# Keeping x by channel through two attention layers: strips and 32x32 turns on VectorE

## The chip, the cores and the metric

The kernel runs on one core of a Trainium2 chip. The metric is the device time of one execution in microseconds (us); before the change the median of 3 runs is 3623.92 us (3623.29 to 3624.22). Engines are named as in the profile: PE is TensorE's matrix multiply and PEld its weight load, DVE is VectorE, ACT is ScalarE, POOL is GpSimd, SP is SyncE, whose queue issues most of the transfers.

## The reference, cut to what matters

x has 128 rows (`s`) of 256 positions with 256 channels, in fp32. Two layers follow one another; each normalizes x in 32 groups of 8 channels over the whole tensor, runs attention within each row, and adds the result to x.

```python
def _gn(v, G=32, eps=1e-5):            # statistics over rows, positions and the 8 channels of a group
    B_, H_, W_, C_ = v.shape
    g = v.reshape(B_, H_, W_, G, C_ // G)
    m = jnp.mean(g, axis=(1, 2, 4), keepdims=True)
    s = jnp.var(g, axis=(1, 2, 4), keepdims=True)
    return ((g - m) / jnp.sqrt(s + eps)).reshape(v.shape)

# layer 0: 8 heads of 32, a bias from pair_repr added after the softmax, and a gate
#   bias = pair_repr @ bias_proj ; gate = sigmoid(xn @ gate_proj) ; q, k, v = xn @ qkv_proj
#   attend = (softmax(q k^T * scale) + bias) v * gate ; out = attend @ out_proj
x = x + _L0_conv_ref(_gn(x), pair_repr, gate_proj, qkv_proj, out_proj, bias_proj)
# layer 1: 4 heads of 64, q, k, v with bias, only keys within 16 positions
#   y = softmax(masked(q k^T / 8)) v @ w_out.T + b_out
x = x + _L1_conv_ref(_gn(x), w_in, b_in, w_out, b_out, 16)
```

The second layer's statistics need all of the first layer's output, so the layers are two passes with x1, the sum after layer 0, kept in DRAM between them.

## The kernel before

The tensors are called here as in the profile: `xg` and `yg` are four rows of x or x1 in SBUF, `px` their transpose in PSUM, `xn` the normalized row by channel, `po` and `1po` the output products, `o` and `1o` the sums that are stored. A prefix `1` marks layer 1.

First comes an early stage: pair_repr is loaded (32 MB), turned and multiplied into the bias table, while all of x (33.5 MB) passes through for the statistics of layer 0. Weights are loaded in one transfer each; w_in and w_out are transposed once on PE.

```python
qkv_sb = const.tile([P, 2, 3 * C], F32, name="qkv_sb")
nc.scalar.dma_start(out=qkv_sb, in_=qkv_w.rearrange("(t p) o -> p t o", p=P))
# ... gate_sb, out_sb the same way, one transfer each; bqk, bv, bo
w_nat = st_pool.tile([P, 8, C], F32, name="w_nat")
nc.scalar.dma_start(out=w_nat[:, 0:6, :], in_=w_in.rearrange("(t p) c -> p t c", p=P))
nc.scalar.dma_start(out=w_nat[:, 6:8, :], in_=w_out.rearrange("(t p) c -> p t c", p=P))
# ... 16 transposes of w_nat on PE into w_in_t, w_out_t; then the loop over pair_repr and x
```

Then each row of each layer. A row arrives with positions on the partitions and must have channels there for the products, so PE transposes it:

```python
def normalized(pool, xg, mean, rstd, name):
    px = proj_bank(f"px{name}")
    for half in range(2):
        for t in range(2):
            nc.tensor.transpose(                                                    # L300
                px[:, half, t * P : (t + 1) * P], xg[:, t, half * P : (half + 1) * P], ident
            )
    xn = pool.tile([P, 2, R], F32, tag="xn", name=f"xn{name}")
    for half in range(2):
        nc.vector.tensor_scalar(                                                    # L305
            xn[:, half, :], px[:, half, :],
            mean[:, half : half + 1], rstd[:, half : half + 1], op0=ALU.subtract, op1=ALU.mult,
        )
    return xn

# by_channel (L317): out[channel, position], weights stationary, xn moving (q, k, gate)
# by_token   (L328): out[position, channel], xn or at stationary, weights moving (v, out)
# each: 4 matmuls 128x128 by 256 columns

def rows(ap, s0, n):                                   # 1 KB pieces: 256 channels of one position
    return ap[s0 : s0 + n].rearrange("s (t p) c -> p s t c", p=P)

# layer 0, in a software pipeline of half rows:
#   even half: scores, q, k of row s+1, normalized(s+2), attend
#   odd half : scores, v, gate of row s+1, finish(s-1), attend
def finish(s):                                         # layer 0
    po = by_token(st[s]["at"], out_sb, 0, f"po{s}")
    # ...
    nc.vector.tensor_tensor(o[:, k], po, xgs[s // XG][:, s % XG], ALU.add)          # L453
    if k == SG - 1:                                    # every 8 rows
        nc.sync.dma_start(out=rows(x1, g * SG, SG), in_=o)
        flat = o.rearrange("p s t c -> p (s t) c")
        for j in range(G):                             # 32 groups
            nc.vector.bn_stats(out=stats1[:, j, g, :], in_=flat[:, :, j * CG : (j + 1) * CG])   # L458
# after the layer: group_columns folds stats1 [P, 32, 16, 6] into mean1, rstd1 (L131 to L170)

def finish(s):                                         # layer 1
    po = by_token(st[s]["at"], w_out_t, 0, f"1po{s}", sim_bank)
    # ...
    nc.vector.tensor_tensor(o[:, k], po, bo.unsqueeze(1).to_broadcast([P, 2, C]), ALU.add)      # L601
    nc.gpsimd.tensor_tensor(o[:, k], o[:, k], xgs[g][:, k], ALU.add)                # L602
    if k == XG - 1:                                    # every 4 rows
        nc.sync.dma_start(out=rows(out[0], g * XG, XG), in_=o)
```

Of the kernel before, what the change touches and what calls it, by code (L numbers as in the profile page):

```python
# [15 lines left out]
P = 128  # L16
# [6 lines left out]
BAND = 16  # L23
KB = 64
# [9 lines left out]
def conv_preact_kernel(  # L34
# [45 lines left out]
    nc.scalar.dma_start(out=bias_w_sb[:, 0:H0], in_=bias_w)  # L80
    qkv_sb = const.tile([P, 2, 3 * C], F32, name="qkv_sb")
    nc.scalar.dma_start(out=qkv_sb, in_=qkv_w.rearrange("(t p) o -> p t o", p=P))
    gate_sb = const.tile([P, 2, C], F32, name="gate_sb")
    nc.scalar.dma_start(out=gate_sb, in_=gate_w.rearrange("(t p) o -> p t o", p=P))
    out_sb = const.tile([P, 2, C], F32, name="out_sb")
    nc.scalar.dma_start(out=out_sb, in_=out_w.rearrange("(t p) o -> p t o", p=P))
# [10 lines left out]
    bo = const.tile([P, C], F32, name="bo")  # L97
    nc.scalar.dma_start(out=bo, in_=b_out.partition_broadcast(P))
# [16 lines left out]
    nc.gpsimd.tensor_copy(seen[KB:P], seen_high[KB:P])  # L115

# [7 lines left out]
    def group_columns(pool, stats, sizes, which):  # L124


        tri = stats.rearrange("p g n (e k) -> p g (n e) k", k=3)
        n, total = tri.shape[2], sum(sizes)
        share = pool.tile([P, n], F32, name=f"share{which}")
        for m, size in enumerate(sizes):  # L130
            nc.gpsimd.memset(share[:, 2 * m : 2 * m + 2], size / (2.0 * total))  # L131
        share = share.unsqueeze(1).to_broadcast([P, G, n])
        dev = pool.tile([P, G, n], F32, name=f"dev{which}")
        nc.vector.tensor_tensor(dev, tri[:, :, :, 1], share, ALU.mult)
        means = pool.tile([P, G], F32, name=f"means{which}")
        nc.vector.tensor_reduce(means, dev, axis=AX.X, op=ALU.add)
        nc.vector.tensor_tensor(dev, tri[:, :, :, 1], means.unsqueeze(2).to_broadcast([P, G, n]), ALU.subtract)
        nc.vector.tensor_tensor(dev, dev, dev, ALU.mult)
        nc.vector.tensor_tensor(dev, dev, share, ALU.mult)
        nc.vector.scalar_tensor_tensor(  # L140
            dev, tri[:, :, :, 2], 1.0 / total, dev, op0=ALU.mult, op1=ALU.add
        )
        within = pool.tile([P, G], F32, name=f"within{which}")
        nc.vector.tensor_reduce(within, dev, axis=AX.X, op=ALU.add)
        ps_m = proj_bank(f"ps_m{which}")
        nc.tensor.matmul(ps_m[:, 0, 0:G], lhsT=avg, rhs=means, start=True, stop=True)
        d = pool.tile([P, G], F32, name=f"d{which}")
        nc.vector.tensor_tensor(d, means, ps_m[:, 0, 0:G], ALU.subtract)
        v = pool.tile([P, G], F32, name=f"v{which}")
        nc.vector.tensor_tensor(v, d, d, ALU.mult)  # L150
        nc.vector.tensor_tensor(v, v, within, ALU.add)
        wide = pool.tile([P, 2, G, CG], F32, name=f"wide{which}")
        nc.vector.tensor_copy(wide[:, 0], means.unsqueeze(2).to_broadcast([P, G, CG]))
        nc.vector.tensor_copy(wide[:, 1], v.unsqueeze(2).to_broadcast([P, G, CG]))
        flat = wide.rearrange("p k g c -> p k (g c)")
        ps_c = proj_bank(f"ps_c{which}")
        for k in range(2):
            for half in range(2):
                nc.tensor.matmul(
                    ps_c[:, 0, 2 * k + half : 2 * k + half + 1],  # L160
                    lhsT=flat[:, k, half * P : (half + 1) * P],
                    rhs=avg[:, 0:1],
                    start=True, stop=True,
                )
        mean = const.tile([P, 2], F32, name=f"mean{which}")
        nc.vector.tensor_copy(mean, ps_c[:, 0, 0:2])
        std = pool.tile([P, 2], F32, name=f"std{which}")
        nc.scalar.activation(std, ps_c[:, 0, 2:4], AF.Sqrt, bias=eps)
        rstd = const.tile([P, 2], F32, name=f"rstd{which}")
        nc.vector.reciprocal(rstd, std)  # L170
        return mean, rstd
# [20 lines left out]
    with ExitStack() as early:  # L192
# [6 lines left out]
        nc.scalar.dma_start(out=w_nat[:, 0:6, :], in_=w_in.rearrange("(t p) c -> p t c", p=P))  # L199
        nc.scalar.dma_start(out=w_nat[:, 6:8, :], in_=w_out.rearrange("(t p) c -> p t c", p=P))  # L200
        for o4 in range(2):
            for kt in range(2):
                pw = proj_bank(f"pw{o4}_{kt}").rearrange("p a b -> p (a b)")
                for j in range(4):
                    nc.tensor.transpose(
                        pw[:, j * P : (j + 1) * P], w_nat[:, 4 * o4 + j, kt * P : (kt + 1) * P], ident
                    )
                if o4 == 0:
                    nc.scalar.copy(w_in_t[:, kt, 0:512], pw)
                else:  # L210
                    nc.scalar.copy(w_in_t[:, kt, 512:768], pw[:, 0:256])
                    nc.scalar.copy(w_out_t[:, kt, :], pw[:, 256:512])
# [82 lines left out]
    def normalized(pool, xg, mean, rstd, name):  # L295

        px = proj_bank(f"px{name}")
        for half in range(2):
            for t in range(2):
                nc.tensor.transpose(  # L300
                    px[:, half, t * P : (t + 1) * P], xg[:, t, half * P : (half + 1) * P], ident
                )
        xn = pool.tile([P, 2, R], F32, tag="xn", name=f"xn{name}")
        for half in range(2):
            nc.vector.tensor_scalar(  # L305
                xn[:, half, :], px[:, half, :],
# [5 lines left out]
    def by_channel(w, col, xn, name):  # L312

        ps = proj_bank(name)
# [8 lines left out]
    def by_token(a, w, col, name, bank=proj_bank):  # L323

        ps = bank(name)
# [7 lines left out]

    def rows(ap, s0, n):
        return ap[s0 : s0 + n].rearrange("s (t p) c -> p s t c", p=P)

    x1 = dram.tile([S, R, C], F32, name="x1")
    SG = min(8, S)
# [5 lines left out]
    with ExitStack() as lay:  # L344
        st1 = lay.enter_context(tc.tile_pool(name="st1", bufs=1))
        stats1 = st1.tile([P, G, S // SG, 6], F32, name="stats1")
        with ExitStack() as lay0:
# [6 lines left out]
            def load(g):  # L354
                if g * XG < S:
                    xg = big.tile([P, XG, 2, C], F32, tag="xg", name=f"xg{g}", bufs=3)
                    nc.sync.dma_start(out=xg, in_=rows(x[0], g * XG, XG))
                    xgs[g] = xg

            def piece(s, n):  # L360
                if s >= S:
                    return
                if n == 0:
                    if s % XG == 0:
                        load(s // XG + 1)
                    st[s] = {"xn": normalized(row, xgs[s // XG][:, s % XG], mean0, rstd0, f"0_{s}")}
# [78 lines left out]
            def finish(s):  # L445
                if s < 0:
                    return
                po = by_token(st[s]["at"], out_sb, 0, f"po{s}")
                g, k = divmod(s, SG)
                if k == 0:  # L450
                    outs[g] = big.tile([P, SG, 2, C], F32, tag="o", name=f"o{g}")
                o = outs[g]
                nc.vector.tensor_tensor(o[:, k], po, xgs[s // XG][:, s % XG], ALU.add)  # L453
                if k == SG - 1:
                    nc.sync.dma_start(out=rows(x1, g * SG, SG), in_=o)
                    flat = o.rearrange("p s t c -> p (s t) c")
                    for j in range(G):
                        nc.vector.bn_stats(out=stats1[:, j, g, :], in_=flat[:, :, j * CG : (j + 1) * CG])  # L458
# [22 lines left out]
        mean1, rstd1 = group_columns(st1, stats1, [SG * 2 * CG] * (S // SG), 1)  # L481
# [4 lines left out]
    with ExitStack() as lay:  # L486
# [6 lines left out]
        def load(g):  # L493
            if g * XG < S:
                xg = big.tile([P, XG, 2, C], F32, tag="xg", name=f"yg{g}")
# [97 lines left out]
        def finish(s):  # L593
            if s < 0:
                return
            po = by_token(st[s]["at"], w_out_t, 0, f"1po{s}", sim_bank)
            g, k = divmod(s, XG)
            if k == 0:
                outs[g] = big.tile([P, XG, 2, C], F32, tag="o", name=f"1o{g}", bufs=2)
            o = outs[g]  # L600
            nc.vector.tensor_tensor(o[:, k], po, bo.unsqueeze(1).to_broadcast([P, 2, C]), ALU.add)  # L601
            nc.gpsimd.tensor_tensor(o[:, k], o[:, k], xgs[g][:, k], ALU.add)  # L602
            if k == XG - 1:
                nc.sync.dma_start(out=rows(out[0], g * XG, XG), in_=o)
# [33 lines left out]
    with tc.If(sure < P):  # L638
        with ExitStack() as lay:
# [12 lines left out]
            stats2 = one.tile([P, G, NX, 6], F32, name="stats2")  # L652
# [57 lines left out]
            def again(layer, s, src, dst, mean, rstd):  # L710
                x2 = two.tile([P, 1, 2, C], F32, tag="x2", name=f"x2_{layer}")
                nc.sync.dma_start(out=x2, in_=src[bass.ds(s, 1)].rearrange("s (t p) c -> p s t c", p=P))
                xn = normalized(two, x2[:, 0], mean, rstd, f"2_{layer}")
# [30 lines left out]
                po = by_token(at, out_sb if layer == 0 else w_out_t, 0, f"po2_{layer}")  # L744
                o = two.tile([P, 1, 2, C], F32, tag="o2", name=f"o2_{layer}")
                nc.vector.tensor_tensor(o[:, 0], po, x2[:, 0], ALU.add)
                if layer == 1:
                    nc.vector.tensor_tensor(o[:, 0], o[:, 0], bo.unsqueeze(1).to_broadcast([P, 2, C]), ALU.add)
                nc.sync.dma_start(out=dst[bass.ds(s, 1)].rearrange("s (t p) c -> p s t c", p=P), in_=o)

            with tc.For_i(0, S, 1) as s:
                again(0, s, x[0], x1, mean0, rstd0)
            for n in range(NX):
                x_stats(stats2, x_load(two, x1, n, "2_"), n)
            mean2, rstd2 = group_columns(one, stats2, [k * CG for k in PARTS], 2)
            with tc.For_i(0, S, 1) as s:
                again(1, s, x1, out[0], mean2, rstd2)
# [25 lines left out]
```

## Time and profile before

| stage | from, to (us) | what it does |
|---|---|---|
| early | 0 to 230 | pair_repr and x pass through; bias table and first statistics |
| layer 0 | 230 to 2331 | 128 rows, 16.21 us for one in the steady stretch |
| between | 2333 to 2360 | statistics of x1, first rows of x1 read back |
| layer 1 | 2360 to 3612 | 128 rows, 9.70 us for one |
| end | 3612 to 3621 | last sums and their store |

The stage limits are read from the timeline; 16.21 us is the distance from one row's q product to the next one's, 9.70 us likewise. A row of the view by groups gives line, engine, operation, output and inputs with their shapes, the number of instructions, then busy time, mean ns of one, and the idle time before them with what ended it. A row of the timeline gives start, length, engine, line and what was done; instructions of one kind in a row are merged, and a bracket gives the idle time before and its releaser. A row of the view by windows gives a stretch, its length, and the busy time of each engine in it, then the granted PE clock, the DMA engines' busy share and GB/s.

### The profile page before, as it was taken

To read this page: it belongs to the slowest core of one execution; us is meant where nothing else is said; L and a number is where in the kernel's file an instruction comes from. 1 tells how busy PE (TensorE), PEld (TensorE's weight loads), DVE (VectorE), ACT (ScalarE), POOL (GpSimd) and SP (SyncE) were. 2 spreads that over 40 slices of the span, in tenths; PEclk is the share of its full clock that TensorE was granted. 3 is DMA by queue.
4 is the path that set the end of the run, shared out by engine and by line. 5 is a ranking of instruction groups with operands and counts; after the bars stand their busy time and mean duration, and the time that the engine had idled before them with its cause. 6 is when DMAs were issued, how large, how long until landed. Compare 5 with 4: busy or idle time off the path is not lost. (4 is left out here: it accounts for less than half of the span.)

```text
span 3621.4 us, 92043 instructions
## 1 busy us (share of the span) xinstructions
PE 3472.4 (96%) x40870; PEld 2703.5 (75%) x40870; DVE 2497.3 (69%) x4353; ACT 1404.4 (39%) x3181; POOL 402.3 (11%) x310
## 2 busy tenths in 40 slices
PE   5769999999999999999999999799999999999998
PEld 4457777777777777777777777488888888888887
DVE  5766776776777677677677677756666666666666
ACT  2334444444444444444444444333333333333332
POOL 0000000000000000000000000023333333333332
PEclk8879999999999999999999999899999999999999
DMA  9930110110111011011011010011211211211211
GB/s 332 350 125 13 48 36 13 48 36 14 47 36 48 13 36 48 13 48 36 13 48 36 15 45 25 25 59 49 72 49 49 72 49 48 72 48 49 72 49 37
DMA packets 154051, 209.85 MB, mean 58 GB/s; under 512 B 2992, under 2 KB 135856, under 8 KB 152496
## 3 DMA queue, kind: packets, MB, share of 16 engines
q1 hardware_dynamic: 150800, 201.34, 17.2%
q8 instruction: 323, 5.29, 0.6%
q10 hardware_dynamic: 2848, 2.56, 0.3%
q14 instruction: 80, 0.66, 0.1%
HBM read 136.78 MB, written 67.11 MB: 56 GB/s over the span
## 5 line engine op out<-in xcount | busy, mean ns | idle before, releaser
L397 ACT ACTIVATE ex<-sim 128x512 f32<-128x512 f32 x1024 | 528.6, 603 | 128.3 <-PE sim L390 127.5
L551 POOL TENSOR_TENSOR 1p<-1ex,seen 128x768 f32<-128x768 f32 x128 | 232.3, 1815 | 2514.0 <-ACT 1ex L549 2514.0
L439 DVE RECIPROCAL d<-d 128x256 f32<-128x256 f32 x256 | 445.8, 1741 | 0.0
L305 DVE TENSOR_SCALAR xn<-px,mean,rstd 128x256 f32<-128x256 f32 x512 | 254.8, 539 | 261.6 <-PE px L300 258.9
L587 DVE RECIPROCAL 1rz<-1z 128x512 f32<-128x512 f32 x128 | 428.1, 3344 | 7.3 <-ACT 1z L585 7.3
L435 DVE TENSOR_TENSOR t<-bv,z 128x256 f32<-128x256 f32 x256 | 108.0, 422 | 460.0 <-ACT z L433 460.0
L433 ACT ACTIVATE z<-avz 128x256 f32<-128x256 f32 x256 | 98.1, 383 | 750.1 <-PE avz L428 740.5
L400 DVE TENSOR_TENSOR both<-ex 128x512 f32<-128x512 f32 x512 | 329.0, 682 | 3.0 <-ACT ex L397 3.0
L390 PE MATMUL sim<-q,k 32*128 32x256 f32 x4096 | 293.3, 400 | 0.0
L415 PE MATMUL avz<-ex,v 128*32 128x256 f32 x4096 | 274.8, 385 | 10.5 <-DVE t L436 10.5
L512 ACT ACTIVATE 1q<-p1q,bqk 128x256 f32<-128x256 f32 x256 | 107.5, 470 | 429.5 <-PE p1q L317 429.5
L422 PE MATMUL bv<-bias_sb,v 128*32 128x256 f32 x4096 | 268.9, 379 | 1.1 <-DVE t L435 1.1
L390 PEld LDWEIGHTS sim<-q,k 32*128 32x128 f32 x4096 | 184.9, 184 | 110.5 <-issue 104.9
L317 PE MATMUL pq<-xn,qkv_sb 128*128 128x256 f32 x1024 | 257.0, 394 | 1.5 <-DVE xn L305 1.4
L328 PE MATMUL pv<-qkv_sb,xn 128*128 128x256 f32 x1024 | 255.1, 392 | 0.0
L328 PE MATMUL po<-out_sb,at 128*128 128x256 f32 x1024 | 247.2, 382 | 6.6 <-DVE at L442 4.9
L520 PEld LDWEIGHTS p1v<-w_in_t,xn 128*64 128x64 f32 x4096 | 221.0, 137 | 42.4 <-issue 42.4
L520 PE MATMUL p1v<-w_in_t,xn 128*64 128x128 f32 x4096 | 251.9, 276 | 0.0
L328 PE MATMUL 1po<-w_out_t,1at 128*128 128x256 f32 x1024 | 243.0, 380 | 3.1 <-DVE 1at L589 3.1
L317 PE MATMUL p1q<-xn,w_in_t 128*128 128x256 f32 x1024 | 243.5, 381 | 0.6 <-DVE xn L305 0.6
L317 PE MATMUL pk<-xn,qkv_sb 128*128 128x256 f32 x1024 | 243.2, 380 | 0.0
L317 PE MATMUL p1k<-xn,w_in_t 128*128 128x256 f32 x1024 | 241.9, 379 | 0.0
(105 smaller groups left out, 5368.0 us busy)
## 6 DMA issues: line engine op xcount, KB each, us to landing
xg<-in_x_dram SPq DMA_DIRECT2D x32, 1024.0 KB, 7.8
x<-o SPq DMA_DIRECT2D x16, 2048.0 KB, 8.4
yg<-x SPq DMA_DIRECT2D x32, 1024.0 KB, 8.9
out_dram<-1o SPq DMA_DIRECT2D x32, 1024.0 KB, 5.3
xs<-in_x_dram SPq DMA_DIRECT2D x7, 4096.0 KB, 20.7
xs<-in_x_dram SPq DMA_DIRECT2D x1, 3072.0 KB, 18.8
xs<-in_x_dram SPq DMA_DIRECT2D x1, 1024.0 KB, 9.7
qkv_sb<-in_L_conv_qkv_proj_dram ACTq DMA_DIRECT2D x1, 768.0 KB, 4.6
```

Source lines behind the costliest of these rows:

```text
L305: nc.vector.tensor_scalar(xn[:, half, :], px[:, half, :], mean[:, half : half + 1], rstd[:, half : half + 1], op0=ALU.subtract, op1=ALU.mult,)
L317: nc.tensor.matmul(ps[:, m, :], lhsT=w[:, kt, col + m * P : col + (m + 1) * P], rhs=xn[:, kt, :], start=(kt == 0), stop=(kt == 1),)
L328: nc.tensor.matmul(ps[:, t, :], lhsT=a[:, kt, t * P : (t + 1) * P], rhs=w[:, kt, col : col + C], start=(kt == 0), stop=(kt == 1),)
L390: nc.tensor.matmul(sims[j][:, kt, :], lhsT=k[p0 : p0 + D0, half, kt * P : (kt + 1) * P], rhs=q[p0 : p0 + D0, half, :], start=True, stop=True,)
L397: nc.scalar.activation(ex[:, j], sims[j], AF.Exp, scale=1.0 / math.sqrt(D0))
L400: nc.vector.tensor_tensor(both[:, j : j + 2], ex[:, j : j + 2, 0, :], ex[:, j : j + 2, 1, :], ALU.add)
L415: nc.tensor.matmul(avz[ps, 0, :], lhsT=v[:, kt, ch], rhs=ex[:, j, kt, :], start=(kt == 0), stop=(kt == 1),)
L422: nc.tensor.matmul(bv0[ps, :], lhsT=v[:, kt, ch], rhs=bias_sb[:, kt, 4 * half + j, :], start=(kt == 0), stop=(kt == 1),)
L439: nc.vector.reciprocal(d, d)
L520: nc.tensor.matmul(ps[KB * half : KB * (half + 1), b, :], lhsT=xn[:, kt, KB * b : KB * (b + 1)], rhs=w_in_t[:, kt, 2 * C + P * half : 2 * ...
L551: nc.gpsimd.tensor_tensor(p.rearrange("p j b q -> p j (b q)"), ex.rearrange("p j b q -> p j (b q)"), seen.rearrange("p b q -> p (b q)").un ...
L587: nc.vector.reciprocal(rz, z)
```

## The change

x is kept with channels on the partitions in both layers. It is loaded in four strips of 64 channels, each to 32 partitions; VectorE turns 32x32 blocks within the strips, after which partition 32a+r holds channels 64a+r (half 0) and 64a+32+r (half 1). The weights' rows are ordered in the same way when they are loaded. Output products come out by channel, so that the residual is added by channel, x1 is stored by channel, and the statistics of layer 1 are one pair of values per partition. Layer 1 loads x1 ready for use; its result is turned back by VectorE before it is stored in strips. The aim is to have no transposes of x on PE. A fallback path that runs only on out-of-range softmax sums is changed in the same way and left out below.

```diff
+A, B = 4, 32
+    def by_strip(ap):
+        return ap.rearrange("(a h r) o -> a r h o", a=A, h=2)
+    def strip(a):
+        return slice(B * a, B * (a + 1))
-    nc.scalar.dma_start(out=qkv_sb, in_=qkv_w.rearrange("(t p) o -> p t o", p=P))
-    nc.scalar.dma_start(out=gate_sb, in_=gate_w.rearrange("(t p) o -> p t o", p=P))
+    for a in range(A):
+        nc.scalar.dma_start(out=qkv_sb[strip(a)], in_=by_strip(qkv_w)[a])
+        nc.scalar.dma_start(out=gate_sb[strip(a)], in_=by_strip(gate_w)[a])
-    nc.scalar.dma_start(out=out_sb, in_=out_w.rearrange("(t p) o -> p t o", p=P))
+    for kt in range(2):
+        for h in range(2):
+            nc.scalar.dma_start(
+                out=out_sb[:, kt, h * P : (h + 1) * P].rearrange("p (a r) -> p a r", a=A),
+                in_=out_w.rearrange("(t p) (a h r) -> t h p a r", p=P, a=A, h=2)[kt, h],
+            )
-    bo = const.tile([P, C], F32, name="bo")           # one transfer, broadcast
+    bo = const.tile([P, 2], F32, name="bo")           # four transfers, one for each strip
-        nc.scalar.dma_start(out=w_nat[:, 0:6, :], in_=w_in.rearrange("(t p) c -> p t c", p=P))
+        for t in range(6):
+            for h in range(2):
+                nc.scalar.dma_start(
+                    out=w_nat[:, t, h * P : (h + 1) * P].rearrange("p (a r) -> p a r", a=A),
+                    in_=w_in.rearrange("(t p) (a h r) -> t h p a r", p=P, a=A, h=2)[t, h],
+                )
...
+    def channel_columns(pool, stats, which):
+        mv = pool.tile([P, 2, 2], F32, name=f"mv{which}")
+        for half in range(2):
+            nc.vector.bn_aggr(out=mv[:, half, :], in_=stats[:, half].rearrange("p n s -> p (n s)"))
+        # ... two products with `within` (1/8 inside a group), six small VectorE operations,
+        # ... a square root and a reciprocal on [P, 2]: mean, rstd
...
-    def normalized(pool, xg, mean, rstd, name):
-        px = proj_bank(f"px{name}")
-        ... four nc.tensor.transpose
+    def normalized(pool, xt, mean, rstd, name):
         for half in range(2):
             nc.vector.tensor_scalar(
-                xn[:, half, :], px[:, half, :],
+                xn[:, half, :], xt[:, half, :],
...
+    def in_strips(ap, s0, n, a):
+        return ap[s0 : s0 + n].rearrange("s (b t) (a c) -> a t (s b) c", t=B, a=A)[a]
+    def turned(dst, src, k):
+        for half in range(2):
+            nc.vector.transpose(
+                out=dst[:, half, :].rearrange("p (b t) -> p b t", t=B),
+                in_=src[:, k * (R // B) : (k + 1) * (R // B), half * B : (half + 1) * B],
+            )
-    x1 = dram.tile([S, R, C], F32, name="x1")
+    x1 = dram.tile([S, 2, P, R], F32, name="x1")
     def rows(ap, s0, n):
-        return ap[s0 : s0 + n].rearrange("s (t p) c -> p s t c", p=P)
+        return ap[s0 : s0 + n].rearrange("s h p q -> p s h q")
# layer 0
-                    nc.sync.dma_start(out=xg, in_=rows(x[0], g * XG, XG))
+                    for a in range(A):
+                        nc.sync.dma_start(out=xg[strip(a)], in_=in_strips(x[0], g * XG, XG, a))
-                    st[s] = {"xn": normalized(row, xgs[s // XG][:, s % XG], mean0, rstd0, f"0_{s}")}
+                    xt = row.tile([P, 2, R], F32, tag="xt", name=f"xt{s}", bufs=5)
+                    turned(xt, xgs[s // XG], s % XG)
+                    st[s] = {"xt": xt, "xn": normalized(row, xt, mean0, rstd0, f"0_{s}")}
-                po = by_token(st[s]["at"], out_sb, 0, f"po{s}")
+                po = by_channel(out_sb, 0, st[s]["at"], f"po{s}")
-                nc.vector.tensor_tensor(o[:, k], po, xgs[s // XG][:, s % XG], ALU.add)
+                nc.vector.tensor_tensor(o[:, k], po, st[s]["xt"], ALU.add)
+                if k % 2 == 1:
+                    for half in range(2):
+                        nc.vector.bn_stats(out=stats1[:, half, s // 2, :], in_=o[:, k - 1 : k + 1, half, :])
-                    for j in range(G):
-                        nc.vector.bn_stats(out=stats1[:, j, g, :], in_=flat[:, :, j * CG : (j + 1) * CG])
# layer 1
-            po = by_token(st[s]["at"], w_out_t, 0, f"1po{s}", sim_bank)
+            po = by_channel(w_out_t, 0, st[s]["at"], f"1po{s}", sim_bank)
-            nc.vector.tensor_tensor(o[:, k], po, bo.unsqueeze(1).to_broadcast([P, 2, C]), ALU.add)
-            nc.gpsimd.tensor_tensor(o[:, k], o[:, k], xgs[g][:, k], ALU.add)
+            for half in range(2):
+                nc.vector.scalar_tensor_tensor(
+                    ot[:, half, :], po[:, half, :], bo[:, half : half + 1], xgs[g][:, k, half, :],
+                    op0=ALU.add, op1=ALU.add,
+                )
+                nc.vector.transpose(
+                    out=outs[g][:, k * (R // B) : (k + 1) * (R // B), half * B : (half + 1) * B],
+                    in_=ot[:, half, :].rearrange("p (b t) -> p b t", t=B),
+                )
-                nc.sync.dma_start(out=rows(out[0], g * XG, XG), in_=o)
+                for a in range(A):
+                    nc.sync.dma_start(out=in_strips(out[0], g * XG, XG, a), in_=outs[g][strip(a)])
```

## The prediction, made before the changed kernel ran

> **What bounds the kernel now.** I read busy time by engine first, then the stretches of the two layers, then the timeline of one row in each, and last the edges between stages.
>
> ```profile
> PE 3472.4 (96%) x40870; PEld 2703.5 (75%) x40870; DVE 2497.3 (69%) x4353; ACT 1404.4 (39%) x3181; POOL 402.3 (11%) x310
> ```
>
> ```profile
> 0.00:200.00 200.00, 128.31 (x864) 90.66 (x864) 128.66 (x398) 56.95 (x98) 5.99 (x38) 0.86 1.03 341
> 230.00:2330.00 2100.00, 2082.67 (x19958) 1506.93 (x19958) 1470.28 (x2908) 926.76 (x2050) 0.00 (x0) 1.00 0.10 31
> 2360.00:3610.00 1250.00, 1243.39 (x19957) 1093.26 (x19957) 853.40 (x894) 415.93 (x1025) 394.10 (x255) 1.00 0.17 53
> ```
>
> Stretch, then PE, PEld, DVE, ACT, POOL, clock, DMA share, GB/s. PE is busy 99% of both layers at full clock; VectorE is at 70% and 68%, DMA at 10% and 17%. The early stage is another matter: DMA is saturated there (share 1.03, 341 GB/s). So in the layers time taken off PE is time off the end, as long as nobody else becomes late; in the early stage only bytes and DMA pauses count.
>
> A busy PE hides gaps between instructions, so I price the transposes from starts. PE's timeline in a layer-0 row, then in a layer-1 row with VectorE's division:
>
> ```profile
> 1006.75 1.89 PE L317 MATMUL pk<-xn,qkv_sb 128*128 128x256 f32 x8
> 1008.48 0.60 PE L300 MATMUL px<-ident,xg 128*128 128x128 f32 x4
> 1009.01 1.07 PE L415 MATMUL avz<-ex,v 128*32 128x256 f32 x16
> ...
> 1015.94 1.89 PE L328 MATMUL po<-out_sb,at 128*128 128x256 f32 x8
> 1017.76 1.07 PE L415 MATMUL avz<-ex,v 128*32 128x256 f32 x16
> ```
>
> ```profile
> 2956.36 0.66 PE L300 MATMUL px<-ident,yg 128*128 128x128 f32 x4
> 2956.86 1.89 PE L328 MATMUL 1po<-w_out_t,1at 128*128 128x256 f32 x8
> ...
> 2961.77 0.68 DVE L589 TENSOR_TENSOR 1at<-1avz,1rz 128x512 f32<-128x512 f32 x1
> ...
> 2964.74 0.79 PE L570 MATMUL 1avz<-1p,1v 64*64 64x80 f32 x32
> ```
>
> From pk to avz is 2.26 us with px between them, from po to avz 1.82 us without: 0.44 us. The even half row (1004.92 to 1012.38) is 7.46 us, the odd one (to 1021.13) 8.75 us; taking po's 1.78 us off the odd one leaves 6.97, so px costs 0.49 us. In layer 1, px start to 1po start is 0.50 us.
>
> Three edges complete the picture: the burst of statistics every 8 rows, the passage between the layers, and the start.
>
> ```profile
> 381.11 6.28 DVE L458 BATCH_NORM_STATS2 stats<-o 128x6 f32<-128x128 f32 x32
> 387.30 0.41 DVE L435 TENSOR_TENSOR t<-bv,z 128x256 f32<-128x256 f32 x1
> 388.43 1.07 PE L415 MATMUL avz<-ex,v 128*32 128x256 f32 x16 [0.62 <-DVE t L436]
> ```
>
> ```profile
> 2331.02 2.07 PE L328 MATMUL po<-out_sb,at 128*128 128x256 f32 x6 [3.08 <-DVE at L442]
> ...
> 2357.95 1.09 PE L300 MATMUL px<-ident,yg 128*128 128x128 f32 x4 [6.27 <-DMA yg<-x]
> 2359.68 3.45 PE L317 MATMUL p1q<-xn,w_in_t 128*128 128x256 f32 x8 [0.64 <-DVE xn L305]
> ```
>
> ```profile
> 5.42 0.38 ACTq L199 DMA_DIRECT2D w_nat<-in_L_conv_w_in_dram  x1
> ...
> 17.38 1.97 PE L205 MATMUL pw<-ident,w_nat 128*128 128x128 f32 x8 [0.70 <-DMA w_nat<-in_L_conv_w_in_dram]
> ```
>
> The burst holds VectorE 6.28 us, `t` comes late and PE waits. Stores of x1 are 130.74 us apart (381.10, 511.84), while 8 rows of 16.21 us are 129.68: 1.06 us lost for each group. Between the layers PE does next to nothing from 2333 to 2359.7. At the start PE, which takes its work in order, waits for w_nat until 17.4 us.
>
> **What the Trainium skill says.** "Perfetto Trace Analysis", Identifying the Most-Contended Engine, warns that matmul busy time misjudges PE and points to weight-load occupancy; here that is 72% and 87% in the layers, and the spacing of starts confirms that PE has no idle time to give. "VectorE: DVE Perf Modes", The three transpose paths: VectorE turns 32x32 blocks only, 311 ns for 128x128 bf16. No run before has such an instruction. The same page, The perf-mode tier table: an fp32 tensor_scalar runs at double rate from SBUF, not from PSUM. The trace has only the PSUM side: L305 takes 539 ns for 256 elements, which agrees with one per cycle. "DMA: Bandwidth & Descriptors", Specifications: line rate wants pieces of 512 B or more. The early stage, mostly 512 B pieces of pair_repr, does move 341 GB/s; nothing here shows 256 B.
>
> **The change, part by part.** Instructions come from the order that the changed program compiles to.
>
> Transposes on PE: 4 for each row and layer go, everything else on PE keeps count and shape (by_channel and by_token both make 4 products of 256 columns). 128 x 0.49 = 62.7 us in layer 0, 128 x 0.50 = 64.0 us in layer 1, all on the path.
>
> VectorE in layer 0. A turn of 256 elements I estimate from the page's 311 ns for 128 and the trace's slope (682 ns for 512 elements at L400, 422 for 256 at L435: 1.02 ns for each): 0.44 us. xn from SBUF: 0.35 us instead of 0.54. Statistics for 512 elements: 277 ns for 128 (L458) and 420 for 256 (L189) give 0.70 us. Per row: two turns +0.88, two xn -0.38, statistics +0.70 - 0.78: +0.42 us on 11.4, so 11.9 of a 15.7 us row. The compiled order puts the turns and the statistics after `o` in the odd half, where VectorE is idle for 2.2 us before `t`; 0.88 + 1.40 in every second row fills that exactly. `both`, the next thing PE needs, has 1.7 us to spare (ends 1025.30, its product starts 1026.97). No new wait. The bursts go: 15 x 1.06 = 16 us.
>
> VectorE in layer 1: xn -0.38; two additions of 0.41 and two turns of 0.44 for one of 0.63: +1.07. 7.4 of 9.2 us. What matters is 1at, which frees the only avz bank: it ends at 2962.45 and the next avz starts at 2964.74, 2.3 us to spare. xn no longer stands between px and the reciprocal, which lets that start 0.7 us earlier; 2.3 + 0.7 - 1.07 - 0.5 (shorter row) leaves 1.4 us. The addition on POOL (1.28 us) was off the path.
>
> Between the layers: 6.28 us of statistics become 1.4, and some 12 us of folding on [128, 1024] become two aggregations and a handful of tiny operations, about 5 us. The store of x1 (8.4 us to landing) then ends last, near 2342 on the old clock; 5.5 us for the first read, no px, xn: p1q at 2348 to 2349, for 2359.7. 11 us saved.
>
> The start gets worse. The ACT queue has 33 transfers instead of 10, and in the compiled program each waits for the completion of the transfer eight places earlier, counted over both queues. That chain runs through the 2 MB loads of pair_repr (landing at some 15 and 21 us) and the first 4 MB of x, which lands near 36; only then do the last twelve, w_nat in 128 B pieces, follow in two rounds of some 4 us. I place w_nat's landing at 45 to 48 us for 17. Behind it PE can't free the first buffer of pair_repr, and SP's third load of it has a completion slot behind a w_nat transfer. So SP has 8 MB in flight by 30 us and the rest at about 50, when the kernel before had moved 8 MB more. DMA bounds this stage, so 8 MB / 341 GB/s = 24 us stay lost.
>
> Small items: first x in 256 B pieces and its turns before xn, +2 us; the last store, 1 MB in four transfers of 256 B pieces, +5 us on the 7.6 us that follow the last sum.
>
> Sum: 3624 - 62.7 - 64 - 16 - 11 + 24 + 2 + 5 = 3501 us.
>
> **Rivals.** (1) The turn is slow on fp32, a microsecond or more. Then layer 1's 1.4 us are used up: at 1.2 us a turn, 1at is about 0.1 us late in each row, and at 2 us 1.7 us, 220 us in all, which would make the change slower. For it: no row of the profile shows the instruction. Against it: VectorE's other rows grow by about 1 ns for an element, with the reciprocal (3344 ns for 512, 1741 for 256) the exception. At twice my estimate, the time is 3510. (2) DMA in 256 B pieces becomes the bound: 4096 pieces in and out for four rows. For it: pieces under 512 B are what the page warns of. Against it: a 1 MB group has 37 to 63 us and lands in 5 to 9 now, with a whole group of lead; it would have to be four times as slow. This leaves only first load and tail, 3500 to 3510. (3) The start is hidden after all, because PE and VectorE catch up faster than DMA: 3480. Or the chain of completions is longer than I see, 50 us instead of 24: 3530.
>
> **Range and chances.** The PE part (127 us) and the bursts are read from starts and are sure to some 10 us unless VectorE is late. The start is the widest term, 0 to 50. Edges may be off by 10. That makes 3470 to 3545. Under 3551 it is faster by over 2%: 0.90. Within 2%: 0.08, with a longer start and a slow turn together. Slower: 0.02, rival (1) at its worst.
>
> **What would show it.** Right: no L300 group; x1 stores some 125.8 us apart (8 x 15.72); output stores 36.8 us apart; no PE wait on `t` in groups of 8; turns near 0.44 us; w_nat's product near 45 us, with a hole in DMA before it; p1q 15 us after the last po. Wrong: a steady PE wait on 1at or `t` (rival 1), on xg or yg (rival 2), a start no longer than before (rival 3).

## The result and the profile after

The changed kernel takes 3515.97 us (median of 4 runs, 3515.41 to 3517.06), the kernel before 3623.61 beside it: a ratio of 0.970, 95% interval 0.969 to 0.972. The prediction was 3501 us with a range of 3470 to 3545.

A total says little about why, so I cut both profiled spans (3621.4 and 3513.7 us) at the same four events and compare piece by piece. The sum of the differences is the whole difference.

| stretch, from the starts and ends of TensorE's products | before | after | difference | predicted |
|---|---|---|---|---|
| start of the span to first pq | 230.06 | 249.98 | +19.9 | +26 |
| layer 0: first pq to end of last po | 2103.03 | 2031.35 | -71.7 | -78.7 |
| end of last po to first p1q | 26.58 | 14.54 | -12.0 | -11 |
| layer 1: first p1q to start of last 1po | 1250.03 | 1202.53 | -47.5 | -64 |
| start of last 1po to the end | 11.69 | 15.29 | +3.6 | +5 |

The stretches of the early stage and of the layers after the change (columns as before: stretch, length, busy time of PE, PEld, DVE, ACT and POOL, clock, DMA share, GB/s):

```profile
0.00:200.00 200.00, 117.62 (x784) 80.58 (x784) 112.31 (x348) 51.82 (x92) 6.98 (x41) 0.91 0.95 307
255.00:2280.00 2025.00, 2017.82 (x19444) 1441.44 (x19443) 1507.35 (x2801) 926.22 (x2049) 0.00 (x0) 1.00 0.17 32
2310.00:3500.00 1190.00, 1182.78 (x19326) 1034.39 (x19325) 921.82 (x1273) 409.95 (x1014) 229.66 (x127) 1.00 0.23 55
```

PE is still 99% busy in both layers, so it is still their bound; VectorE has risen to 74% and 77%, DMA to 17% and 23%. The early stage moves 307 GB/s where it moved 341. Over 200 us that is 6.8 MB less, and 6.8 MB at 341 GB/s are 20 us: the whole loss of the first stretch. It falls in the first 60 us, which move 215 GB/s instead of 331; from 60 to 200 us it is 346 for 345.

PE's timeline of one row of layer 0, then of layer 1. Each line is start, duration, then who did what:

```profile
384.98 1.89 PE L387 MATMUL pk<-xn,qkv_sb 128*128 128x256 f32 x8
386.80 1.07 PE L488 MATMUL avz<-ex,v 128*32 128x256 f32 x16
...
393.73 1.89 PE L387 MATMUL po<-at,out_sb 128*128 128x256 f32 x8
395.55 1.07 PE L488 MATMUL avz<-ex,v 128*32 128x256 f32 x16
```

```profile
2905.37 0.79 PE L643 MATMUL 1avz<-1p,ones 64*64 64x80 f32 x32
2906.09 1.99 PE L387 MATMUL 1po<-1at,w_out_t 128*128 128x256 f32 x8
2907.92 1.89 PE L387 MATMUL p1q<-xn,w_in_t 128*128 128x256 f32 x8
```

The px lines are gone. In layer 0 pk to avz is 1.82 us where it was 2.26, as expected from po to avz. In layer 1 look at 1po: from its start to p1q it is 1.83 us, while before the change it was 1.72 (2956.86 to 2958.58), for the same eight products:

```profile
2958.58 1.89 PE L317 MATMUL p1q<-xn,w_in_t 128*128 128x256 f32 x8
```

A row takes 9.31 us instead of 9.70: 0.39 saved, not the 0.50 that lay between px and 1po.

VectorE's timeline at the end of a group of eight rows in layer 0, where the burst of statistics was:

```profile
396.38 1.29 DVE L529 BATCH_NORM_STATS2 stats<-o 128x6 f32<-128x512 f32 x2
397.58 0.75 DVE L377 STREAM_TRANSPOSE xt<-xg 128x256 f32<-128x256 f32 x2
398.54 0.43 DVE L508 TENSOR_TENSOR t<-bv,z 128x256 f32<-128x256 f32 x1 [0.20 <-ACT z L506]
```

The statistics and the turns fit between `o` and `t`; `t` now waits for ScalarE, not for VectorE. The stores of x1 are 126.17 us apart (396.38, 522.55), which is 8 rows of 15.77 us with nothing lost.

PE's timeline between the layers and at the start:

```profile
2279.12 2.21 PE L387 MATMUL po<-at,out_sb 128*128 128x256 f32 x6 [3.08 <-DVE at L515]
2295.88 3.78 PE L387 MATMUL p1q<-xn,w_in_t 128*128 128x256 f32 x8 [6.55 <-DVE xn L362]
```

```profile
38.20 0.47 PE L264 MATMUL pw<-ident,w_nat 128*128 128x128 f32 x1 [19.71 <-DMA w_nat<-in_L_conv_w_in_dram]
...
53.96 1.54 PE L264 MATMUL pw<-ident,w_nat 128*128 128x128 f32 x6 [0.25 <-DMA w_nat<-in_L_conv_w_out_dram]
55.30 1.91 PE L300 MATMUL pz<-ident,pr 128*128 128x128 f32 x8
```

From 18.5 to 55.3 us PE does nothing but wait for the pieces of w_nat and turn them as they land. The SyncE queue has the matching hole: after its third transfer it issues nothing until 41.86.

```profile
10.22 7.90 SPq L237 DMA_DIRECT2D xs<-in_x_dram  x1
41.86 18.45 SPq L287 DMA_DIRECT2D pr<-in_L_conv_pair_repr_dram  x2
```

### The profile page after: what moved, and what is told of

Same layout as the page of the kernel before. It is cut to its first block, busy times and chain, and to the rows that moved or that the text cites. A ratio compares the mean times of both kernels' runs of the same rounds, so it can differ in the third digit from the quotient of the medians.

```text
span 3513.7 us, 90334 instructions
## 1 busy us (share of the span) xinstructions
PE 3364.5 (96%) x39840; PEld 2590.5 (74%) x39840; DVE 2595.0 (74%) x4605; ACT 1403.8 (40%) x3183; POOL 238.4 (7%) x169
## 3 DMA queue, kind: packets, MB, share of 16 engines
q1 hardware_dynamic: 350480, 201.35, 23.5%
## 5 line engine op out<-in xcount | busy, mean ns | idle before, releaser
L660 DVE RECIPROCAL 1rz<-1z 128x512 f32<-128x512 f32 x128 | 429.2, 3353 | 193.1 <-ACT 1z L658 193.1
L387 PE MATMUL 1po<-1at,w_out_t 128*128 128x256 f32 x1024 | 258.3, 396 | 2.9 <-DVE 1at L662 2.9
L585 ACT ACTIVATE 1q<-p1q,bqk 128x256 f32<-128x256 f32 x256 | 107.3, 470 | 381.6 <-PE p1q L387 381.6
L387 PE MATMUL po<-at,out_sb 128*128 128x256 f32 x1024 | 243.3, 380 | 4.9 <-DVE at L515 4.9
L387 PE MATMUL pg<-xn,gate_sb 128*128 128x256 f32 x1024 | 241.9, 379 | 0.0
```

What stands on the lines that cost most here:

```text
L387: nc.tensor.matmul(ps[:, m, :], lhsT=w[:, kt, col + m * P : col + (m + 1) * P], rhs=xn[:, kt, :], start=(kt == 0), stop=(kt == 1),)
L660: nc.vector.reciprocal(rz, z)
```

## The experiments

My theory: (a) the layers gain TensorE time alone, less than four transposes show by their spacing, because the first weight load behind a group of small tiles is now paid by a product; (b) layer 0 also gains what its bursts cost; (c) the start loses by the queue of weight transfers on ScalarE; (d) VectorE and DMA stay off the path. The rivals stand in each expectation. Differences are against the changed kernel's 3515.97 us; the kernel before, run beside each experiment, was 3623.0 to 3623.2. All times are medians.

**The transposes put back, all else as changed** (in both layers, result unused):

```diff
                     turned(xt, xgs[s // XG], s % XG)
+                    px = proj_bank(...)
+                    for hh in (0, 1):
+                        for tt in (0, 1):
+                            nc.tensor.transpose(px[:, hh, tt * P : (tt + 1) * P], xt[:, hh, tt * P : (tt + 1) * P], ident)
```

> The changed kernel with the four TensorE transposes per row put back in both layers, at the place they had before; nothing reads their result. Theory (the layers gain TensorE time alone, 0.43 us per row in layer 0 and 0.39 in layer 1): 128 x (0.43 + 0.39) = 105 us come back, about 3621 us, row periods of 16.2 and 9.70 us again. Rival (the gain is VectorE's, or comes from xn no longer waiting for TensorE): nothing comes back beyond what TensorE can hide, within 15 us of 3516.

Measured: 3620.56 us, +104.6 (ratio to before 0.999, interval 0.9985 to 0.9998). Layer 0 takes 2087.12 us by the same events, +55.8, layer 1 1251.42, +48.9. So TensorE's transposes account for 0.44 and 0.38 us per row. PE's timeline in layer 1:

```profile
2959.10 0.66 PE L586 MATMUL px<-ident,yg 128*128 128x128 f32 x4
2959.59 1.89 PE L387 MATMUL 1po<-1at,w_out_t 128*128 128x256 f32 x8
2961.32 1.89 PE L387 MATMUL p1q<-xn,w_in_t 128*128 128x256 f32 x8
```

1po to p1q is 1.73 us again. Layer 1 had gained 47.5, so it leaves nothing for another cause. Layer 0 had gained 71.7: 15.9 us of that are not transposes.

**One transpose of four put back, in layer 1 alone:**

```diff
+                xr = xgs[s // XG][:, s % XG]
+                px = proj_bank(f"px1_{s}")
+                nc.tensor.transpose(px[:, 0, 0:P], xr[:, 0, 0:P], ident)
                 st[s] = {"xn": normalized(row, xgs[s // XG][:, s % XG], mean1, rstd1, f"1_{s}")}
```

> The changed kernel with one of the four transposes per row put back, in layer 1 alone, ahead of the next row's first product. Theory (each transpose costs about 0.12 us of TensorE, but the first instruction after the group of small tiles pays about 0.1 us that the transposes used to pay): 0.02 us per row, so 0 to +4 us, 3516 to 3520. Rival (each transpose is a quarter of the row's 0.39 us): 128 x 0.10 = +12.5 us, about 3528.

Measured: 3523.93 us, +8.0 (ratio 0.973, interval 0.971 to 0.974): 0.06 us per row, between theory and rival. PE's timeline, then PE's weight loads in the same row:

```profile
2956.34 0.33 PE L582 MATMUL px<-ident,yg 128*128 128x128 f32 x1
2956.50 1.89 PE L387 MATMUL 1po<-1at,w_out_t 128*128 128x256 f32 x8
2958.23 1.89 PE L387 MATMUL p1q<-xn,w_in_t 128*128 128x256 f32 x8
```

```profile
2956.33 0.14 PEld L582 LDWEIGHTS px<-ident,yg 128*128 128x128 f32 x1
2956.34 1.65 PEld L387 LDWEIGHTS 1po<-1at,w_out_t 128*128 128x128 f32 x8
```

1po's weights load from 2956.34, 0.16 us before 1po starts, and 1po to p1q is 1.73 us again instead of 1.83. In the changed kernel the load starts with the product, at 2906.09, so nothing before it hides it:

```profile
2906.09 1.59 PEld L387 LDWEIGHTS 1po<-1at,w_out_t 128*128 128x128 f32 x8
```

So the single transpose costs 0.16 us (px to 1po) and gives 0.10 back. The exposed load is as large as I said; the transpose is dearer than the 0.12 I expected. With all four, px to 1po is 0.50, so the other three cost 0.11 each, and 0.06 + 3 x 0.11 = 0.39, the row's saving. Why the first of them costs 0.05 us more than the others is not shown.

**The burst of statistics put back.** A first form gathers the eight statistics instructions of a group at its end:

```diff
-                if k % 2 == 1:
-                    for half in range(2):
-                        nc.vector.bn_stats(out=stats1[:, half, s // 2, :], in_=o[:, k - 1 : k + 1, half, :])
+                if k == SG - 1:
+                    for j in range(1, SG, 2):
+                        for half in range(2):
+                            nc.vector.bn_stats(out=..., in_=o[:, j - 1 : j + 1, half, :])
```

> The changed kernel with the statistics of layer 0 taken after each eighth row in one burst of eight instructions of 0.69 us (5.5 us), instead of two after every second row. Theory (part of layer 0's gain is that such bursts no longer stop TensorE once in eight rows): 16 bursts of 1.0 to 1.5 us lost, +16 to +24 us, about 3532 to 3540. Rival (the bursts were always hidden behind TensorE): within 4 us of 3516.

Measured: 3515.83 us, -0.1 (ratio 0.970, interval 0.969 to 0.972). This tells nothing of bursts: the compiled order moved each pair back to where its two rows are ready, and the trace shows pairs, as in the changed kernel. The second form makes every instruction read all eight rows:

```diff
-        stats1 = st1.tile([P, 2, S // 2, 6], F32, name="stats1")
+        stats1 = st1.tile([P, 2, 2 * S, 6], F32, name="stats1")
...
+                    for j in range(16):
+                        for half in range(2):
+                            nc.vector.bn_stats(out=stats1[:, half, g * 16 + j, :], in_=o[:, :, half, j * 16 : (j + 1) * 16])
```

> The changed kernel with the statistics of layer 0 taken as before the change: after each eighth row, 32 instructions of 128 elements, each of which reads all eight rows, so that none can be done earlier. Theory (such a burst of 6.3 us makes t late by about 1 us in each group of eight rows): the stores of x1 are 127.2 us apart instead of 126.17, +15 to +18 us in layer 0. Rival (the 16 us of layer 0 that the transposes don't explain have another source): 126.2 apart, nothing lost in layer 0. In both cases the aggregation between the layers gets four times as many entries, an estimated 11 us more (1.8 us for each half now). In all +26 to +29 us, about 3543, or about 3527.

Measured: 3551.42 us, +35.4 (ratio 0.980, interval 0.979 to 0.982). VectorE's and PE's timelines after the first group's end:

```profile
394.85 5.87 DVE L530 BATCH_NORM_STATS2 stats<-o 128x6 f32<-128x128 f32 x30
400.63 0.41 DVE L508 TENSOR_TENSOR t<-bv,z 128x256 f32<-128x256 f32 x1
400.96 0.41 DVE L511 SCALAR_TENSOR_TENSOR d<-e,z 128x256 f32<-128x256 f32 x1
401.29 0.42 DVE L509 TENSOR_TENSOR t<-avz,t 128x256 f32<-128x256 f32 x1
```

```profile
398.81 1.89 PE L387 MATMUL pk<-xn,qkv_sb 128*128 128x256 f32 x8
401.85 1.07 PE L488 MATMUL avz<-ex,v 128*32 128x256 f32 x16 [1.15 <-DVE t L509]
```

The wait of avz on `t` is back, 1.15 us; the stores are 127.42 us apart and layer 0 takes 2048.48 us, +17.1. That is the missing 15.9, within 1.2 us. Between the layers it loses 15.5 us more: the two aggregations take 14.01 us instead of 3.62, which I had estimated, and the last burst 6.27 instead of 1.29, which I had left out. The profiled execution is the shortest of the four, 3547.67 us; the 4 to 6 us by which the others are longer are not explained.

**The start: fewer transfers, input weights first.**

```diff
-        for t in range(6):
-            for h in range(2):
-                nc.scalar.dma_start(out=w_nat[:, t, ...], in_=w_in...[t, h])
+        w_raw = st_pool.tile([P, 6, C], F32, name="w_raw")
+        nc.scalar.dma_start(out=w_raw, in_=w_in.rearrange("(t p) c -> p t c", p=P))
+        for h in range(2):
+            nc.vector.tensor_copy(<w_nat, half h in the order of strips>, <w_raw>)
...
+            if m == 8:
+                weights()        # qkv, gate, out_sb and the biases: issued here, not at the top
```

> The changed kernel with the input weights fetched first, in 2 transfers instead of 13 (two VectorE copies put the channels in order afterwards), and the other weights' transfers issued 8 steps into the loop of the bias stage. Theory (the start's 20 us are the wait of that loop for the end of a queue of 33 transfers on ScalarE): 15 to 20 us less, about 3497 to 3501, and the bias stage's second step starts near 22 us instead of 55. Rival (the 20 us are the DMA engines' time for small pieces, which is only moved): within 5 us of 3516.

Measured: 3501.63 us, -14.3 (ratio 0.9665, interval 0.965 to 0.968). PE's timeline of the start:

```profile
7.00 1.94 PE L267 MATMUL pw<-ident,w_nat 128*128 128x128 f32 x8 [7.00 <-DVE w_nat L258]
15.98 2.61 PE L303 MATMUL pz<-ident,pr 128*128 128x128 f32 x11 [7.05 <-DMA pr<-in_L_conv_pair_repr_dram]
18.39 1.78 PE L267 MATMUL pw<-ident,w_nat 128*128 128x128 f32 x8
20.00 1.58 PE L303 MATMUL pz<-ident,pr 128*128 128x128 f32 x13
```

w_nat is there at 7 us, the bias stage goes on at 20.0 instead of 55.3, and the first pq starts at 235.90: 14.1 of the 19.9 us come back, 5.8 don't. The edit changes three things at once: the number of transfers, their size and their order. The next run changes the order alone.

**The start: the same 33 transfers, the 13 of w_nat issued first** (the diff only moves the lines).

> The changed kernel with the same 33 weight transfers on ScalarE, the 13 of the input weights issued ahead of the other 20. Theory (the wait is for the last of the queue's transfers, whichever it is, since ScalarE does no other work till all are issued): 0 to -5 us, 3511 to 3516. Rival (the wait is for the input weights' own place in the queue): -10 to -15 us, about 3501 to 3506.

Measured: 3506.11 us, -9.9 (ratio 0.968, interval 0.966 to 0.969): the rival's lower end. But the trace shows part of the theory too. Its timeline of ScalarE and PE:

```profile
45.24 1.28 ACT L271 ACT_TABLE_LOAD   x1 [45.24 <-DMA bo<-in_L_conv_b_out_dram]
46.53 1.07 ACT L271 COPY w_in_t<-pw 128x512 f32<-128x512 f32 x2
47.17 1.97 PE L267 MATMUL pw<-ident,w_nat 128*128 128x128 f32 x8 [29.08 <-ACT w_in_t L271]
```

Half of w_nat had gone through PE by 15.2 us, and still PE stood for 29 us from 18.1: ScalarE, which has to empty PE's bank, issues the other transfers first and does its first work at 45. PE's wait is now named for ScalarE and ends at 47 instead of 54. Both the place in the queue and its length count.

**VectorE's room in layer 1.** The output turns done a second time, then three times more, into a tile that nobody reads:

```diff
+                for more in range(1):      # 3 in the second run
+                    junk = row.tile([P, R // B, B], F32, tag="junk", ...)
+                    nc.vector.transpose(out=junk, in_=ot[:, half, :].rearrange("p (b t) -> p b t", t=B))
```

> The changed kernel with each of layer 1's two output turns per row done a second time, into a tile that nobody reads: 0.86 us more VectorE work per row. Theory (VectorE has about 1.8 us to spare between its last result of a row and the next use): 0 to +2 us, 3516 to 3518. Rival (VectorE is the bound of layer 1 once TensorE is relieved): up to 128 x 0.86 = +110 us.

Measured: 3517.46 us, +1.5 (ratio 0.971, interval 0.969 to 0.973). A second set of turns is free.

> The changed kernel with each of layer 1's output turns done four times: 2.5 us more VectorE work per row, more than the 1.8 us to spare. Theory: the loop from one row's normalisation through VectorE to the next becomes the bound, 0.5 to 0.7 us more per row, +65 to +90 us, about 3580 to 3605. Rival (more room than 1.8 us, because the order of VectorE's work gives way): under +10 us.

Measured: 3623.93 us, +108.0 (ratio 1.000, interval 0.999 to 1.001); layer 1 alone takes 1309.84, +107.3 or 0.84 us per row. So the room ends between one extra set of turns and three, but the loss is larger than the expected 0.5 to 0.7 us per row. The groups of VectorE in layer 1, with the turns four times, name a second cause (busy time and mean ns of one stand behind the bar):

```profile
L685 DVE STREAM_TRANSPOSE junk<-1ot 128x256 f32<-128x256 f32 x696 | 243.4, 396 | 0.0
L362 DVE TENSOR_SCALAR xn<-yg,mean,rstd 128x256 f32<-128x256 f32 x236 | 217.1, 959 | 0.0
```

and the same group in the changed kernel:

```profile
L362 DVE TENSOR_SCALAR xn<-yg,mean,rstd 128x256 f32<-128x256 f32 x250 | 90.9, 406 | 0.0
```

xn, the same instruction on the same data, takes 959 ns instead of 406. The timeline of one row, all engines:

```profile
2957.99 1.81 POOL L624 TENSOR_TENSOR 1p<-1ex,seen 128x768 f32<-128x768 f32 x1 [8.46 <-ACT 1ex L622]
2958.30 1.98 DVE L362 TENSOR_SCALAR xn<-yg,mean,rstd 128x256 f32<-128x256 f32 x2
...
2960.20 3.34 DVE L660 RECIPROCAL 1rz<-1z 128x512 f32<-128x512 f32 x1
```

The pair of xn, 0.73 us elsewhere, begins 0.3 us after GpSimd's 1p and lasts until 1p is done plus one xn: it is the first xn of each pair that waits and takes 1.4 to 1.7 us in the steady rows; the second, which the next expectation names, takes 0.40. In the changed kernel xn starts at 2904.78 and is over before 1p starts at 2906.07. Two things in the traces that run beside 1p and are not slowed narrow the cause: before the change xn, read from PSUM, starts within 1p in every row from 2404 to 3578 us and takes 536 to 545 ns, and in the changed kernel the reciprocal takes 3353 ns beside 1p, and 3339 without it in the run with four turns. The next run takes xn off VectorE.

**The turns four times, xn of layer 1 on ScalarE:**

```diff
-                st[s] = {"xn": normalized(row, xgs[s // XG][:, s % XG], mean1, rstd1, f"1_{s}")}
+                for half in range(2):
+                    nc.scalar.activation(xn[:, half, :], xgs[s // XG][:, s % XG, half, :], AF.Identity,
+                                         bias=shift1[:, half : half + 1], scale=rstd1[:, half : half + 1])
```

> The kernel with layer 1's turns done four times, with the normalisation xn of layer 1 on ScalarE instead of VectorE. With the turns four times, the second xn of a row took up to 2.03 us instead of 0.41, while GpSimd's product 1p was running. Theory (xn on VectorE waits for GpSimd, 1.6 us of the row): VectorE's row falls from 10.15 to about 9.8, where the loop from 1avz to 1at ends, so 45 to 70 us less than with xn on VectorE, about 3555 to 3580. Rival (xn is slow for another reason, or the row is set by the sum of VectorE's other work): only xn's own 0.7 us or less is felt unevenly, within 20 us of 3624.

Measured: 3567.95 us, 56.0 less than with xn on VectorE (ratio to before 0.985, interval 0.983 to 0.987). The row is 9.68 us and VectorE 87% busy, so the sum of its work is not what holds it; the loop is. One round of it, from 1avz to the next:

```profile
2956.71 0.84 PE L652 MATMUL 1avz<-1p,1v 64*64 64x80 f32 x32
...
2958.98 3.35 DVE L669 RECIPROCAL 1rz<-1z 128x512 f32<-128x512 f32 x1 [1.23 <-ACT 1z L667]
...
2965.59 0.66 DVE L671 TENSOR_TENSOR 1at<-1avz,1rz 128x512 f32<-128x512 f32 x1
2966.39 0.84 PE L652 MATMUL 1avz<-1p,1v 64*64 64x80 f32 x32
```

The reciprocal waits for 1z, which ScalarE reads from 1avz; from there to the end of 1at, at 2966.25, VectorE has no pause, and 0.14 us later the next 1avz starts. In the changed kernel the same stretch takes 7.5 us, from a 1avz (2904.77) to the end of the 1at that frees its bank (2902.98 plus a row of 9.31); six more turns at about 0.35 us in a run make 9.6. They add 2.1 us and the row grows by 0.37, so the room was about 1.7 us. What the row had above 9.68 went with xn, so it was xn's wait and its consequences.

**Smaller pieces:** x loaded and the output stored in pieces of 128 B, twice as many transfers:

```diff
-                        nc.sync.dma_start(out=xg[strip(a)], in_=in_strips(x[0], g * XG, XG, a))
+                        for h in range(2):
+                            nc.sync.dma_start(out=xg[strip(a)][:, :, h * B : (h + 1) * B],
+                                              in_=in_strips(x[0], g * XG, XG, a)[:, :, h * B : (h + 1) * B])
```

> The changed kernel with x loaded and the output stored in pieces of 128 B instead of 256 B, in twice as many transfers. Theory (the DMA engines, 0.17 and 0.23 busy, are hidden in both layers): 0 to +5 us, 3516 to 3521, the rest being the first load and the last store. Rival (the smaller pieces already hold the layers back): +20 us or more.

Measured: 3518.73 us, +2.8 (ratio 0.971, interval 0.9695 to 0.973). Layer 1 takes 1202.88 us, unchanged; in the profiled execution the first pq starts 1.5 us later and the last 1po is 2.6 us farther from the end. Even at half the size the pieces are hidden within the layers; at the two ends they are not.

**A version on top of the lean start:** out_w too in one transfer of whole rows, and the last group of the output stored in three parts:

```diff
+            parts = {XG - 1: (0, XG)}
+            if g == S // XG - 1:
+                parts = {XG // 2 - 1: (0, XG // 2), XG - 2: (XG // 2, XG - 1 - XG // 2), XG - 1: (XG - 1, 1)}
```

> The lean start, with the output weights too fetched in one transfer of whole rows (two VectorE copies put the channels in order), and the last four rows of the output stored in three parts (two rows, one, one) as they are done. Theory: the last store carries a quarter of its bytes, 2 to 4 us less at the end; the start, 5.8 us later than in the kernel before, gains 1 to 3 us if 2048 pieces of 128 B were what still held it: 3494 to 3499. Rival (the rest of the start is not the pieces): the start stays at 236 us for the first product, about 3499.

Measured: 3495.11 us (ratio 0.965, interval 0.963 to 0.966), 6.5 less than the lean start and the fastest of all. Last 1po to the end is 11.58 us instead of 14.91 in the lean start, and the first pq starts at 233.58, 2.3 us earlier. The early stage of this version:

```profile
0.00:200.00 200.00, 130.25 (x842) 91.67 (x842) 129.80 (x400) 55.45 (x98) 7.41 (x41) 0.82 1.02 332
```

## Where the prediction was right and where it was wrong

The direction and the account by stages held, and the time came out 15 us above the prediction. Adding the table's differences from the predicted terms: start -6, layer 0 +7, between the layers -1, layer 1 +16.5, end -1.4. That the total came so near is in part luck: the gain of the layers was put 23.5 us too high, and the loss at the start 6 us too high.

**Transposes on PE: right in kind, mis-sized; this is the term that was off.** "128 x 0.49 = 62.7" and "128 x 0.50 = 64.0" were to be 127 us "sure to some 10"; they are 55.8 and 48.9. In layer 0 I had two readings, 0.44 from pairs of starts and 0.49 from half rows, and took the larger. It rested on "taking po's 1.78 us off the odd one"; eight products in a run take 1.73 (pk to px in the profile before), so the half row without px is 7.02, not 6.97. In layer 1 I read px to 1po and took it for what goes when px goes. That ignores who pays for the first weight load: 0.10 us of it came back on 1po, 13 us over the layer, as the single transpose shows. The 2 to 4 us that are left of the 16.5 are not resolved.

**Bursts: right.** 16 predicted, 15.9 left over when the transposes are accounted for, 17.1 when the burst is put back.

**VectorE: right where it matters.** A turn takes 420 ns for 0.44 predicted, statistics of 512 elements 686 for 0.70. xn takes 406 ns for 0.35: from SBUF it is a quarter faster than the 539 from PSUM. The Trainium skill, "VectorE: DVE Perf Modes", The perf-mode tier table, gives an fp32 `tensor_scalar` double rate from SBUF. At the 1.02 ns per element that the prediction took from the trace, this would save 131 ns on 256 elements, an estimate, and 133 are measured; but a single size can't tell a higher rate from a shorter fixed part, so the rate is not shown. 1at ended 1.8 us before the next 1avz (2902.98, 2904.77) for 1.4 predicted, and the doubled turns were free. Rival (1), a slow turn, is out; the run with four shows that six more turns in a row would have cost 108 us.

**The start: right in mechanism.** w_nat's products came from 38 to 55 us, the last of them after the "45 to 48"; the queue of SyncE had its hole, and 6.8 MB stayed behind for the 8 I priced. The lean start gives 14.1 of 19.9 us back. What I did not see is the second half of that chain: ScalarE itself does no work until its last transfer is issued, at 44.9 us. Of the 5.8 us left, 2.3 went with out_w's four transfers of 128 B pieces. The other 3.5 were not tried. The first 60 us move 290 GB/s in the lean start and 306 in the last version, at a DMA share of 0.97 and 0.98, where the kernel before moved 331 at 1.01. So what is left looks less like another hole than like DMA time that brings fewer bytes while the weights are fetched; which transfer takes it is not shown.

**Between the layers and the end: right**, -12.0 for -11 and +3.6 for +5. The DMA rival (2) is out: neither 256 B nor 128 B pieces hold the layers. Rival (3) is out too: the start was neither hidden nor 50 us longer.

## What to carry to other kernels

Price a removed instruction by the spacing of starts around it and also around the instruction that inherits its place: the first weight load after a group of small tiles goes to whoever comes first. An engine's room is what its loop leaves and not only its idle share, and a move within it can push an instruction into another engine's time. When a layout change splits weight loads into many transfers, fetch whole rows and reorder on chip; a queue of an engine that is not needed early might do as well, which was not tried.

## What was not expected of the hardware

VectorE's xn, now read from SBUF, and GpSimd's 1p don't run at the same time: moved onto each other, the pair of xn took 1.98 us instead of 0.73 and waited for 1p's end. The Trainium skill has this in "SBUF — State Buffer", Who interferes with whom: a two-port VectorE operation and a GpSimd operation block each other fully, and the first to issue goes first; the trace agrees, in that 1p had begun 0.3 us earlier and the first xn ended 0.15 us after it. That xn runs as a two-port operation is not itself shown. Before the change xn read PSUM, so the new layout brought the risk with it, and only the order of VectorE's work keeps it out.

Aggregation of statistics is not tiny: 1.85 us for 384 numbers per partition and 7.0 us for 1536. And a transfer of x with 1024 pieces of 128 B lands in 4.3 us, one with 1024 pieces of 256 B in 5.8 (medians from issue to landing): half the bytes take three quarters of the time.
